# A macaron layer on one core: the planner counts GpSimd's own lengths and turns of two lengths, masks move to VectorE, and the maxima's transposition moves within bare turns

## The chip, the cores and the metric

The kernel runs on one core of a Trainium2 chip, as one launch. The metric is the device time in microseconds. The kernel before took 1269.98 us (median of three runs, 1268.98 to 1270.04). Engines are named as in the profile: PE (matmuls), DVE (VectorE), ACT (ScalarE), POOL (GpSimd) and SP, which here only issues DMAs.

## The reference, cut to what matters

```python
def ffn(x):                       # on 2*1024 tokens of 512
    logits = x @ W_router.T       # 8 experts, best two, weights normalized
    h = einsum('td,erd->ter', x, lora_A)                  # rank 16
    return x @ W_base.T + b_base + einsum('ter,eor,te->to', h, lora_B, w) * 2.0

def bitnet_linear(x, weight, scale):
    s = max(mean(abs(weight), axis=1), 1e-8)
    y = einsum('bsi,oi->bso', x, sign(weight / s[:, None]))
    return nan_to_num(y * (s * scale), nan=0.0, posinf=1e6, neginf=-1e6)

def attn(x):                      # 32 heads, 8 key/value heads, head width 16
    q, k, v = (bitnet_linear(x, ...) for each)
    return bitnet_linear(softmax(q k^T / 4) v, o_weight, o_scale)

x = x + 0.5 * ffn(layernorm(x))
x = x + attn(layernorm(x))
x = x + 0.5 * ffn(layernorm(x))
```

x is 2 x 1024 x 512, all in float32. `nan_to_num` follows each of the four projections. It is computed exactly by `finite`: two clamps, their sum, a mask "y times 0 equals 0" that is false where y is not finite, and a copy of y where the mask is true.

## The kernel before, in words

The tokens of each of the two batches fall into two groups of 512, each four tiles of 128. A group (b, g) goes through a chain of steps: layernorm and transposition (`ln_T`), router and low-rank part, base matmuls (`ffn_tiles`), a second layernorm, the projections (`qkv_part`: i = 0 to 3 are q, 4 is k, 5 is v). q and k go to DRAM as a high and a low part (`qd`, `kd`, stored from L572), v stays in SBUF (`vd`). After attention a group is divided by its sums (`normalize`), projected (`o_proj`) and goes through the second `ffn`. `binarize` makes the weights' signs.

Attention has 32 units: a batch, a block of 512 queries and a key/value head with its four query heads. Each unit takes four **turns**. A turn does, for three successive stages at once, 8 score tiles for the row maxima (m; each a matmul of L776 and a DVE maximum of L784), 8 score tiles for the exponentials (e0 and e1; L811 and L815 on PE, then L818 on ACT) and four pieces of the product with v (A0 to A3; L851). The e tiles of a unit begin five turns after its m tiles. In the first turn after a unit's maxima are complete, `m_place` (the entry S) transposes them on PE (mp, L796), splits them into a high and a low part on DVE (mT, L798 and L799) and sends both over SP into `mq` (L802), which e1 reads (L815) from the next turn on. After the first turn of a unit, `place` loads the next unit's q (k<-qd, L725) and k (k<-kd, L733); that data is used four turns later.

All instructions are put out by one Python program, whose order is the order on every engine. The **planner**, `Flow`, keeps a clock `flow.t` in ticks of 0.115 us. The steps of the groups and the weights are generators, **strands**. A strand yields what it needs next: a kind (P, v, a, g for PE, DVE, ACT, POOL, d for a DMA on SP, r for buffers, u and j for conditions) and the kind of the piece before it. `go` sets its due time `s.at`: the end of the piece before, plus a distance from the table `LATER`, such as gv=30 for DVE after POOL or av=16 for DVE after ACT. `offer(kind)` places the first strand whose piece of that kind is due, in order of rank, unless the engine is still held (`busy`, set ahead by `LASTS` at the ends and by `APART` inside attention; 11 and 10 ticks for POOL).

During attention a turn follows a written order: `LEAD_IN` at first, `FULL` where a PE piece of a strand is due (37 entries, two F entries for such pieces), `BARE` where none is (35 entries and no F). V and W offer DVE, C and D ACT; POOL and SP are offered after every entry, but SP not before S in a turn that has one. Each turn counts `TICK` = 64 ticks. Where something must be done before work goes on, `need` runs `until`: each tick it clears the holds and offers all engines, with no attention work between, till the condition holds. `need` stands before each `place` and asks for the q and k of that unit; for the first unit of batch 1 that is at the end of turn 60. Here this is called the flush. After attention the strands that are left are played out with the table for free engines.

Of the kernel before, what the change touches and what calls it, by code (L numbers as in the profile page):

```python
# [32 lines left out]
def macaron_kernel(ctx: ExitStack, tc: tile.TileContext, x_in, wbT, b_base, wrT, aT, bT,  # L33
# [82 lines left out]
    for t in mqs:  # L116
# [4 lines left out]

    TICK = 64
    LATER = {False: dict(Pv=10, Pa=10, PP=0, vP=36, aP=36, gP=40, va=20, av=16, vg=16, ag=14, gv=30,
                         ga=30, gg=0, vv=0, aa=0, dv=50, dg=50, da=50, dd=0, gd=32, vd=26, ad=26,
                         xd=50, dP=60),
# [1 line left out]
                        gg=0, vv=0, aa=0, dv=26, dg=26, da=26, dd=0, gd=13, vd=8, ad=8, xd=26,  # L129
                        dP=30)}  # L130
    LASTS = dict(P=9, v=6, a=5, g=11, d=5)
    APART = dict(P=0, v=5, a=5, g=10, d=5)

    class Strand:
# [4 lines left out]
    class Flow:  # L139
        def __init__(self):  # L140
            self.t, self.free, self.strands, self.n = 0, True, [], 0
            self.stock = dict(m=3, n=4, t=11, xT=2, xL=2, hT=1, fb=6)
            self.lock = None
            self.busy = dict.fromkeys("Pvagd", 0)

        def spawn(self, gen, rank):
            self.n += 1
# [6 lines left out]
        def go(self, s):  # L154

            if s.kind in LASTS:
                s.last, s.end = s.kind, self.t
            w = next(s.gen, None)
            if w is None:
                s.done = True  # L160
                self.strands.remove(s)
                return
            s.kind, s.arg = w[0], w[1]
            if s.kind in LASTS:
                since = w[2] if len(w) > 2 and w[2] is not None else s.end
                s.banks = w[3] if len(w) > 3 else 0
                s.at = since + LATER[self.free].get(s.arg + s.kind, 0) if s.arg else since
# [30 lines left out]
        def offer(self, kind):  # L198
            if self.t < self.busy[kind]:
                return False  # L200
            self.settle()
            for s in self.strands:
                if s.kind == kind and s.at <= self.t and (
                        kind != "P" or self.lock in (None, s) and s.banks <= self.stock["fb"]):
                    if kind == "P":
                        self.lock = None
                        self.stock["fb"] -= s.banks
                    self.go(s)
                    self.busy[kind] = self.t + (LASTS if self.free else APART)[kind]
                    self.settle()  # L210
                    return True
            return False
# [22 lines left out]
    def finite(y, o, n, fast, back):  # L235


        yield "r", dict(m=1)
        lo = t512(f"lo{n}")
        m = tmp.tile([P, 512], mybir.dt.uint8, tag="mask", name=f"m{n}", bufs=3)  # L240
        lo_, m_ = lo[:, :], m[:, :]
        if len(o.shape) == 3:
            lo_, m_ = (v.rearrange("p (a c) -> p a c", a=o.shape[1]) for v in (lo_, m_))
        src, t = back
        if fast:
            yield "v", src, t
            nc.vector.tensor_scalar(lo_, y, 0.0, -BIG, ALU.min, ALU.max)
            yield "v", "v"
            nc.vector.tensor_scalar(o, y, 0.0, BIG, ALU.max, ALU.min)
            e, eng = ("v", nc.vector) if fast > 1 else ("g", nc.gpsimd)  # L250
            yield e, "v"
            eng.tensor_tensor(o, o, lo_, ALU.add)
            last = e, flow.t
            yield "v", ""
            nc.vector.tensor_scalar(m_, y, 0.0, 0.0, ALU.mult, ALU.is_equal)
        else:
            yield "g", src, t
            nc.gpsimd.tensor_scalar(lo_, y, 0.0, -BIG, ALU.min, ALU.max)  # L258
            yield "g", ""
            nc.gpsimd.tensor_scalar(m_, y, 0.0, 0.0, ALU.mult, ALU.is_equal)  # L260
            yield "g", ""
            nc.gpsimd.tensor_scalar(o, y, 0.0, BIG, ALU.max, ALU.min)
            yield "g", "g"
            nc.gpsimd.tensor_tensor(o, o, lo_, ALU.add)  # L264
            last = "g", flow.t
        flow.give(t=1)
        yield ("v", *last)
        nc.vector.copy_predicated(o, m_, y)  # L268
        flow.give(m=1)
# [9 lines left out]
    def ln_T(xt, n, mv, given, tiles, xs, rank):  # L279


        xT, xL = xs if len(xs) > 1 else (xs[0], None)
        own = slice(tiles[0], tiles[-1] + 1)
        yield "u", lambda: given >= set(tiles)
        yield "v", "v"
        ve = sm.tile([P, TG], F32, tag="ve", name=f"ve{n}{tiles[0]}")
        nc.vector.tensor_scalar(ve[:, own], mv[:, own, 1], EPS, None, ALU.add)
        yield "g", "v"
        rstd = sm.tile([P, TG], F32, tag="rstd", name=f"rstd{n}{tiles[0]}", bufs=4)
        nc.gpsimd.tensor_tensor(rstd[:, own], ve[:, own], mhalf[:, own], ALU.pow)  # L290
        calm = not flow.free
        if calm:
            yield "g", ""
            neg = sm.tile([P, TG], F32, tag="neg", name=f"neg{n}{tiles[0]}", bufs=4)
            nc.gpsimd.tensor_tensor(neg[:, own], mv[:, own, 0], rstd[:, own], ALU.mult)
            yield "g", ""
            nc.gpsimd.tensor_scalar(neg[:, own], neg[:, own], -1.0, None, ALU.mult)
        at = flow.t

        def part(t):  # L300
            yield "r", dict(t=1)
            yield "a" if calm else "v", "g", at
            xn = t512(f"xn{n}_{t}")
            if calm:
                nc.scalar.activation(xn, xt[:, t, :], AF.Identity, bias=neg[:, t:t + 1],
                                     scale=rstd[:, t:t + 1])
            else:
                nc.vector.tensor_scalar(xn, xt[:, t, :], mv[:, t, 0:1], rstd[:, t:t + 1],
                                        ALU.subtract, ALU.mult)
            yield "P", "a" if calm else "v", None, 1  # L310
            pt = bank(f"pt{n}_{t}").rearrange("p (c q) -> p c q", c=KC)
            for c in range(KC):
                nc.tensor.transpose(pt[:, c, :], xn[:, c * P:(c + 1) * P], ident)
            flow.give(t=1)
            yield "a", "P"
            tok = slice(t * P, (t + 1) * P)
            nc.scalar.copy(xT[:, :, tok], pt)
            if xL is not None:
                yield "v", "a"
                nc.vector.tensor_tensor(xL[:, :, tok], pt, xT[:, :, tok].bitcast(F32), ALU.subtract)  # L320
            flow.give(fb=1)

        yield "j", [flow.spawn(part(t), rank) for t in tiles]
# [146 lines left out]
    def binarize(w, n_out, name, sc, rank, at):  # L470
# [18 lines left out]
            nc.vector.reciprocal(rs[:, c * P:(c + 1) * P], s[:, c * P:(c + 1) * P])  # L489
        wr = const.tile([P, KC, n_out], F32R, name=f"sign_{name}")  # L490
        for c in range(KC):
            yield "g", "v" if c == 0 else "g"
            nc.gpsimd.tensor_tensor(w[:, c, :], w[:, c, :], rs[:, 0:n_out], ALU.mult)
            g = flow.t
            if c:
                yield "a", "g", was
                nc.scalar.activation(wr[:, c - 1, :], w[:, c - 1, :], AF.Sign)
            was = g
# [149 lines left out]
    def o_proj(b, g, hs, rank, mv, given, fast=False):  # L648
# [5 lines left out]
        def part(t):  # L654
# [20 lines left out]
                yield "g", "a"  # L675
                nc.gpsimd.tensor_tensor(y, y, osc, ALU.mult)
            r = t512(f"ro{n}_{t}")
            yield from finite(y[:, :], r[:, :], f"o{n}_{t}", fast, ("v" if fast else "g", flow.t))
            yield "v" if fast else "g", "v"
            (nc.vector if fast else nc.gpsimd).tensor_tensor(xt[:, t, :], xt[:, t, :], r, ALU.add)  # L680
            flow.give(t=2)
# [5 lines left out]
        for t in range(TG):  # L687
# [10 lines left out]
    FULL = ("V F W m0(3) e0(4) e0(7) e0(1) m0(7) e1(4) e1(7) e1(1) A0 A1 S C e0(5) e0(3) e1(5) "  # L698
            "e0(2) m0(4) V e1(2) m0(0) e1(3) A2 A3 m0(2) e0(0) C e0(6) m0(5) e1(6) e1(0) m0(6) D "
            "m0(1) F")  # L700
    BARE = ("A0 A1 S e0(1) C m0(7) e1(1) e0(3) e0(4) e0(2) m0(0) e1(3) e1(2) C e1(4) m0(2) m0(5) A2 "
            "A3 m0(3) e0(0) V e0(6) D e1(0) e0(7) e0(5) e1(6) m0(1) e1(7) V e1(5) W m0(6) m0(4)")
    LEAD_IN = ("m0(0) m0(5) m0(2) V m0(7) F C V m0(4) m0(1) V F C m0(6) V F C V m0(3) V S F C V")
    FULL, BARE, LEAD_IN = (
# [50 lines left out]
    def place_v(u):  # L755

        b, _, g = units[u]
        v = p2.tile([P, NT, 32], F32, tag="vaug", name=f"vaug{u}", bufs=3)
        nc.gpsimd.memset(v[:, :, HD:32], 1.0)
        nc.gpsimd.tensor_copy(v[:, :, 0:HD], vd[b][:, :, g * HD:(g + 1) * HD])  # L760
        st[u]["v"] = v
# [99 lines left out]

    def attention(chains, n0):

        start = flow.t
        flow.free, flow.lock = False, None
        flow.busy = dict.fromkeys("Pvagd", flow.t)
        flow.stock["fb"] -= 4
# [14 lines left out]
            raise RuntimeError([(s.rank, s.kind, s.arg) for s in flow.strands])  # L882

        for n in range(n0, TU * len(units) + LEAD + 1):
            begin = flow.t = max(flow.t, start + (n - n0) * TICK)
            m, e, a = todo(n, 0), todo(n, LEAD), todo(n, LEAD + 1)
            live = [c for c in live if not c.done]
            while chains and len(live) < 3 and chains[0][0] <= n:
# [1 line left out]
            if e and e[1] == 0:  # L890
                need(*[(units[e[0]][0], h, KC + 1) for h in range(NG)])
                place_v(e[0])
            order = (LEAD_IN if not e and not a else FULL if flow.wants("P", begin + at_F)
                     else BARE)

            hold = n % TU == 0 and n // TU
            for pos, (kind, p, i) in enumerate(order):
                flow.t = max(flow.t, begin + pos * TICK // len(order))
                if kind == "m":
                    if m:  # L900
                        m_tile(m[0], m[1] * 2 * REP + i)
# [25 lines left out]
            if m and m[0] + 1 < len(units) and (m[1] == 0 or n == n0):  # L927
                b, qb, g = units[m[0] + 1]
                need((b, qb, g // 2), *[(b, h, KC) for h in range(NG)])
                place(m[0] + 1)  # L930
        flow.free = True
        flow.stock["fb"] += 4
        flow.busy = dict.fromkeys("Pvagd", flow.t)

# [51 lines left out]

    def chain_o():
        yield from binarize(wraw["o"], D, "o", osc, 8, usec(36))
        load_x(1, 1)

    def have(*keys):
# [67 lines left out]
```

## Time and profile before

| | |
|---|---|
| median of three runs | 1269.98 us (1268.98 to 1270.04) |
| profiled execution | 1269.39 us, span 1267.6 us |
| mean granted PE clock | 0.923 |
| instructions | 21528 |
| HBM read, written | 51.19 MB, 25.94 MB |
| m, e and av tiles' matmuls (L776, L811, L815, L851) | 367.2, 284.8, 261.4, 284.7 us busy |
| DVE maxima (L784) | 649.7 us, 1024 of 682 ns |
| ACT exponentials (L818) | 543.8 us, 1024 of 604 ns |

A row of the groups gives line, engine, operation, result and source, shapes and count, then busy time, the mean of one in ns, and the idle time just before it with what ended it. A busy PE is modelled and includes its pipelining. In the slices a digit is tenths of a fortieth of the span, 31.7 us. The chain that ended last is followed back from the last instruction to whatever released each step.

### The profile page before, as it was taken

How to read it: one execution, taken by the hardware profiler on the slowest of the kernel's cores; microseconds unless marked ns; L12 is line 12 of the kernel's file. 1: busy time of each engine (PE TensorE's matmuls, PEld its weight loads, DVE VectorE, ACT ScalarE, POOL GpSimd, SP SyncE). 2: the span in 40 equal slices, each digit the busy share in tenths (PEclk: the TensorE clock that was granted, in tenths of full speed). 3: DMA queues.
4: the chain of work that ended last, by engine and by line, in shares of the span. 5: the costliest groups of instructions: out<-in, count | busy, mean ns of one | idle time of the engine just before them, and what ended most of it. 6: DMA issues, size and time to landing. Idle time of an engine off the chain costs nothing.

```text
span 1267.6 us, 21528 instructions
## 1 busy us (share of the span) xinstructions
PE 1085.7 (86%) x8453; PEld 599.8 (47%) x8453; DVE 857.5 (68%) x1644; ACT 666.3 (53%) x1305; POOL 400.2 (32%) x387
## 2 busy tenths in 40 slices
PE   3977368999999999988658898999998799989868
PEld 3535234555454554444434454544455345545434
DVE  6575646787777777776245885787778567785373
ACT  2221135776567566656245575656575466677501
POOL 4232954300110271040785603471110030921201
PEclk8988568999999999999869898999999899999889
DMA  7011113211111122122113122111112211111111
GB/s 251 1 63 46 44 43 115 85 52 48 45 47 47 44 84 68 43 71 84 51 44 107 56 75 81 48 42 59 54 52 69 79 67 52 61 52 45 42 35 41
DMA packets 43089, 79.04 MB, mean 62 GB/s; under 512 B 7259, under 2 KB 10331, under 8 KB 42987
## 3 DMA queue, kind: packets, MB, share of 16 engines
q1 hardware_dynamic: 41578, 74.97, 16.9%
q10 hardware_dynamic: 1152, 2.10, 0.4%
q8 instruction: 67, 1.10, 0.4%
q0 software_dynamic: 256, 0.59, 0.3%
q14 instruction: 36, 0.29, 0.1%
HBM read 51.19 MB, written 25.94 MB: 61 GB/s over the span
## 4 chain that ended last, share of the span: by engine, by line
PE 59%; DMA 12%; DVE 11%; issue 8%; POOL 5%; SPq 2%; ACT 2%; POOLq 0%; DVEq 0%; ACTq 0%
PE av L851 16%; PE m L776 13%; PE e L811 8%; DMA k<-kd 8%; PE e L815 6%; DVE mn L784 4%; PE pbf L438 4%; PE pbs L438 3%; PE po L663 2%; POOL ma L260 1%; PE pq L532 1%; ACT es L818 1%; DMA an<-ad 1%; DMA x<-in_x 1%; SPq L725 1%
## 5 line engine op out<-in xcount | busy, mean ns | idle before, releaser
L784 DVE TENSOR_REDUCE mn<-m 128x1 f32<-128x512 f32 x1024 | 649.7, 682 | 244.5 <-PE e L815 100.8
L818 ACT ACTIVATE es<-e 128x512 f32<-128x512 f32 x1024 | 543.8, 604 | 343.1 <-PE e L815 295.1
L776 PE MATMUL m<-k 64*128 64x512 f32 x1024 | 367.2, 450 | 75.2 <-DMA k<-kd 40.6
L811 PE MATMUL e<-k 64*128 64x512 f32 x1024 | 284.8, 454 | 22.6 <-ACT es L818 20.0
L851 PE MATMUL av<-es,vaug 128*32 128x256 f32 x4096 | 284.7, 397 | 20.2 <-issue 8.0
L776 PEld LDWEIGHTS m<-k 64*128 64x128 f32 x1024 | 173.3, 193 | 219.6 <-DVE mn L784 81.9
L815 PE MATMUL e<-mq,two_r 64*128 64x512 f32 x1024 | 261.4, 407 | 2.5 <-DMA mq<-mT 2.5
L851 PEld LDWEIGHTS av<-es,vaug 128*32 128x32 f32 x4096 | 110.1, 111 | 156.6 <-issue 103.6
L811 PEld LDWEIGHTS e<-k 64*128 64x128 f32 x1024 | 123.7, 191 | 78.8 <-DVE mn L784 30.6
L815 PEld LDWEIGHTS e<-mq,two_r 64*128 64x128 f32 x1024 | 149.6, 193 | 15.8 <-POOL ma L260 2.9
L615 POOL TENSOR_TENSOR an<-an,rb 128x512 f32<-128x512 f32 x15 | 19.6, 1308 | 175.7 <-DMA rb<-rd 140.3
L438 PE MATMUL pbf<-wb,xTf 128*128 128x512 f32 x128 | 65.0, 638 | 0.0
L453 POOL TENSOR_TENSOR x<-x,hbf 128x512 f32<-128x512 f32 x8 | 10.2, 1280 | 164.7 <-ACT hbf L450 164.7
L438 PE MATMUL pbs<-wb,xTs 128*128 128x512 f32 x128 | 61.4, 606 | 0.1
L433 POOL TENSOR_TENSOR x<-x,bh 128x512 f32<-128x512 f32 x32 | 40.9, 1304 | 0.0
L258 POOL TENSOR_SCALAR loa<-y 128x512 f32<-128x512 f32 x17 | 12.9, 762 | 88.3 <-ACT y L537 87.7
L438 PEld LDWEIGHTS pbf<-wb,xTf 128*128 128x128 f32 x128 | 24.3, 202 | 28.7 <-issue 27.5
L565 POOL TENSOR_TENSOR z<-z,y 128x512 fp32r<-128x512 f32 x17 | 21.6, 1274 | 49.8 <-ACT y L562 47.2
L268 DVE COPY_PREDICATED z<-ma,y 128x512 f32<-128x512 uint8 x20 | 19.0, 950 | 25.4 <-POOL z L264 25.2
L438 PEld LDWEIGHTS pbs<-wb,xTs 128*128 128x128 f32 x128 | 22.7, 189 | 27.3 <-issue 26.4
L453 POOL TENSOR_TENSOR x<-x,hbs 128x512 f32<-128x512 f32 x8 | 10.3, 1282 | 79.4 <-ACT hbs L450 79.4
L562 ACT CAST y<-z 128x512 fp32r<-128x512 f32 x20 | 12.5, 623 | 41.6 <-DVE z L268 40.3
(210 smaller groups left out, 1098.7 us busy)
## 6 DMA issues: line engine op xcount, KB each, us to landing
k<-qd SPq DMA_DIRECT2D x128, 128.0 KB
k<-kd SPq DMA_DIRECT2D x31, 512.0 KB
ad<-avs SPq DMA_DIRECT2D x32, 256.0 KB
x<-in_x SPq DMA_DIRECT2D x16, 256.0 KB
qd<-y SPq DMA_DIRECT2D x16, 256.0 KB
qd<-z SPq DMA_DIRECT2D x16, 256.0 KB
an<-ad SPq DMA_DIRECT2D x15, 256.0 KB
rb<-rd SPq DMA_DIRECT2D x15, 256.0 KB
```

The costliest lines, as they stand in the source:

```text
L433: nc.gpsimd.tensor_tensor(xt[:, t, :], xt[:, t, :], bh, ALU.add)
L438: nc.tensor.matmul(pb, xT[:, c, t * P:(t + 1) * P], wb[:, c, :], start=(c == 0), stop=False)
L453: nc.gpsimd.tensor_tensor(xt[:, t, :], xt[:, t, :], hb, ALU.add)
L565: (nc.vector if fast else nc.gpsimd).tensor_tensor(lo, o, y, ALU.subtract)
L615: nc.gpsimd.tensor_tensor(z, z, rb, ALU.mult)
L663: nc.tensor.matmul(po, hs[j][:, c, t * P:(t + 1) * P], wo[:, c, :], start=(c + j == 0), stop=(c + j == KC))
L776: nc.tensor.matmul(s["m", i], s["q"][rows_of(h), h % 2, qt * P:(qt + 1) * P], s["k"][rows_of(h), kh * 512:(kh + 1) * 512], start=True, sto ...
L784: nc.vector.tensor_reduce(s["mn"][:, h, qt, kh:kh + 1], s.pop(("m", i)), AX.X, ALU.max, negate=True)
L811: nc.tensor.matmul(t, s["k"][rows_of(h), kt * P:(kt + 1) * P], s["q"][rows_of(h), h % 2, :], start=True, stop=False)
L815: nc.tensor.matmul(t, two_r[rows_of(h), h % 2, :], s["mq"][rows_of(h), :], start=False, stop=True)
L818: nc.scalar.activation(e, s.pop(("e", i)), AF.Exp, scale=HD ** -0.5)
L851: nc.tensor.matmul(s["av"][32 * h:32 * h + 32, cols], s["v"][:, kt, :], s["es"][kt * REP + h][:, cols], start=(kt + half == 0), stop=(kt + ...
```

## The change

1. The planner counts POOL's queue. `Flow.pool` is the tick at which all that is placed on POOL has ended. Every POOL piece adds its own length, given as a fourth value of its yield (6, 17, 9, 3, 4), else `SUM` = 11. The strand's own end becomes `pool - SUM`, and POOL is offered again only when `pool` is reached. The distances of later pieces (`last`, `at`, `g`) count from there too.
2. In `finite`, where it isn't one of the fast forms, the mask moves from POOL to DVE and stands between the two clamps in the strand's order.
3. A bare turn counts `BRIEF` = 50 ticks; full and leading turns keep 64. Each turn's begin follows from the one before, and not from the number of the turn; after attention the clock is set to the last turn's end.
4. In `BARE`, S moves from the third to the seventeenth entry.
5. `chain_o` yields for a place on SP before it loads the x of group (1, 1).

```diff
-    TICK = 64
+    TICK, BRIEF = 64, 50
...
+    SUM = 11
...
+            self.pool = 0
...
             if s.kind in LASTS:
                 s.last, s.end = s.kind, self.t
+            if s.kind == "g":
+
+                self.pool = max(self.pool, self.t) + (s.banks or SUM)
+                s.end = self.pool - SUM
...
-                    self.busy[kind] = self.t + (LASTS if self.free else APART)[kind]
+                    self.busy[kind] = (self.pool if kind == "g" else
+                                       self.t + (LASTS if self.free else APART)[kind])
...
-            last = e, flow.t
+            last = e, flow.t if e == "v" else flow.pool - SUM
...
-            yield "g", src, t
+            yield "g", src, t, 6
             nc.gpsimd.tensor_scalar(lo_, y, 0.0, -BIG, ALU.min, ALU.max)
-            yield "g", ""
-            nc.gpsimd.tensor_scalar(m_, y, 0.0, 0.0, ALU.mult, ALU.is_equal)
-            yield "g", ""
+            yield "v", src, t
+            nc.vector.tensor_scalar(m_, y, 0.0, 0.0, ALU.mult, ALU.is_equal)
+            yield "g", "", None, 17
             nc.gpsimd.tensor_scalar(o, y, 0.0, BIG, ALU.max, ALU.min)
             yield "g", "g"
             nc.gpsimd.tensor_tensor(o, o, lo_, ALU.add)
-            last = "g", flow.t
+            last = "g", flow.pool - SUM
...
-        yield "g", "v"
+        yield "g", "v", None, 9
         rstd = sm.tile([P, TG], F32, tag="rstd", name=f"rstd{n}{tiles[0]}", bufs=4)
...
-            yield "g", ""
+            yield "g", "", None, 3
             neg = sm.tile([P, TG], F32, tag="neg", name=f"neg{n}{tiles[0]}", bufs=4)
...
-        at = flow.t
+        at = flow.pool - SUM
...
-            yield "g", "v" if c == 0 else "g"
+            yield "g", "v" if c == 0 else "g", None, 11 if n_out > P else 4
             nc.gpsimd.tensor_tensor(w[:, c, :], w[:, c, :], rs[:, 0:n_out], ALU.mult)
-            g = flow.t
+            g = flow.pool - SUM
...
-    BARE = ("A0 A1 S e0(1) C m0(7) e1(1) e0(3) e0(4) e0(2) m0(0) e1(3) e1(2) C e1(4) m0(2) m0(5) A2 "
+    BARE = ("A0 A1 e0(1) C m0(7) e1(1) e0(3) e0(4) e0(2) m0(0) e1(3) e1(2) C e1(4) m0(2) m0(5) S A2 "
             "A3 m0(3) e0(0) V e0(6) D e1(0) e0(7) e0(5) e1(6) m0(1) e1(7) V e1(5) W m0(6) m0(4)")
...
         v = p2.tile([P, NT, 32], F32, tag="vaug", name=f"vaug{u}", bufs=3)
+        flow.pool = max(flow.pool, flow.t) + 5
...
-        start = flow.t
+        begin, span = flow.t, 0
...
-            begin = flow.t = max(flow.t, start + (n - n0) * TICK)
+            begin = flow.t = max(flow.t, begin + span)
...
+            span = BRIEF if order is BARE else TICK
...
-                flow.t = max(flow.t, begin + pos * TICK // len(order))
+                flow.t = max(flow.t, begin + pos * span // len(order))
...
         flow.free = True
+        flow.t = begin + span
...
         yield from binarize(wraw["o"], D, "o", osc, 8, usec(36))
+        yield "d", "x"
         load_x(1, 1)
```

More of the change, by code (lines that the diff above doesn't have):

```diff
@@ L292, in ln_T @@
         if calm:
-            yield "g", ""
+            yield "g", "", None, 3
             neg = sm.tile([P, TG], F32, tag="neg", name=f"neg{n}{tiles[0]}", bufs=4)
             nc.gpsimd.tensor_tensor(neg[:, own], mv[:, own, 0], rstd[:, own], ALU.mult)
-            yield "g", ""
+            yield "g", "", None, 3
             nc.gpsimd.tensor_scalar(neg[:, own], neg[:, own], -1.0, None, ALU.mult)
-        at = flow.t
+        at = flow.pool - SUM
         def part(t):
@@ L677, in part @@
             r = t512(f"ro{n}_{t}")
-            yield from finite(y[:, :], r[:, :], f"o{n}_{t}", fast, ("v" if fast else "g", flow.t))
+            yield from finite(y[:, :], r[:, :], f"o{n}_{t}", fast,
+                              ("v" if fast else "g", flow.t if fast else flow.pool - SUM))
             yield "v" if fast else "g", "v"
```

## The prediction

> **What bounds the kernel now.** I read the page first, then the chain that ended last, then that chain and the POOL queue in the two stretches where the 40 slices dip, and last the rows of the operations that the change moves. The page's busy shares and slices:
>
> ```profile
> PE 1085.7 (86%) x8453; PEld 599.8 (47%) x8453; DVE 857.5 (68%) x1644; ACT 666.3 (53%) x1305; POOL 400.2 (32%) x387
> PE   3977368999999999988658898999998799989868
> DVE  6575646787777777776245885787778567785373
> POOL 4232954300110271040785603471110030921201
> ```
>
> PE is busy 86%, and in long stretches all the time; there a cheaper POOL is worth nothing. PE falls to 3 to 6 tenths in slices 5 and 6 and again around slices 20 and 21, and exactly there POOL reads 9, 5, 8, 5. POOL's 32% over the whole span hides two stretches in which it is the bound. The same by stage (columns: PE, PEld, DVE, ACT, POOL busy, clock, DMA):
>
> ```profile
> 100.00:170.00 70.00, 37.61 (x159) 24.38 (x160) 38.34 (x66) 9.52 (x18) 46.84 (x35) 0.67 0.13 43
> 170.00:546.00 376.00, 359.09 (x3011) 193.20 (x3010) 280.43 (x516) 238.23 (x460) 78.19 (x84) 0.96 0.17 60
> 546.00:660.00 114.00, 79.93 (x610) 46.17 (x604) 58.77 (x99) 53.17 (x100) 62.36 (x50) 0.82 0.19 63
> 660.00:1180.00 520.00, 471.69 (x4091) 257.78 (x4091) 378.93 (x704) 323.00 (x630) 166.56 (x159) 0.96 0.18 63
> ```
>
> PE lacks 32 us in 100 to 170, 34 us in 546 to 660 and 48 us in 660 to 1180. In the second of these the chain that ended last runs through POOL, one `finite` after another (start, length, what):
>
> ```profile
> 615.45 1.95 POOL ma L260
> 617.47 1.93 POOL z L262
> 619.48 1.29 POOL z L264
> 620.85 1.13 POOL loa L258
> 622.04 1.93 POOL ma L260
> ...
> 641.62 1.93 POOL ma L260
> 643.61 1.92 POOL z L262
> 645.62 1.27 POOL z L264
> 646.91 1.77 DVE z L268
> ```
>
> This is the flush: after turn 60 `need` wants k and q of batch 1, and the planner puts all of their remaining pieces ahead of turn 61. DVE's copy and ACT's next work stand in order behind POOL, so PE gets nothing. From 120.06 to 141.58 the chain holds four more masks; the SP queue, which must then send q to DRAM, issues unit 1's k at 146.90 and that lands 20.7 us later. So nine masks lie on the path, 1.4% of the span (17.5 us). The rows that the change moves:
>
> ```profile
> L260 POOL TENSOR_SCALAR ma<-y 128x512 uint8<-128x512 f32 x17 | 32.9, 1935 | 1.0
> L260 POOL TENSOR_SCALAR mo<-yo 128x512 uint8<-128x512 f32 x12 | 23.2, 1934 | 0.6
> L255 DVE TENSOR_SCALAR ma<-y 128x512 uint8<-128x512 f32 x3 | 1.2, 415 | 0.0
> L796 PE MATMUL mp<-ident,mm 128*16 128x128 f32 x32 | 9.5, 297 | 13.9 <-DVE mm L789 13.9
> ```
>
> **The masks.** With the four of `vd`, 33 masks leave POOL: 33 x 1.935 = 63.9 us. They cost DVE 33 x 0.415 = 13.7 us. POOL's part of a `finite` shrinks from 0.61 + 1.93 + 1.92 + 1.27 = 5.73 to 3.80 us. Only masks on the path count: four at the start, five in the flush.
>
> Against the full 1.93 stands a rule of the Trainium skill, SBUF — State Buffer, section "Who interferes with whom": a VectorE tensor_scalar from SBUF to SBUF in its two-port mode and a GpSimd instruction exclude each other, and whichever comes second waits for the whole of the first. The trace has such meetings: the DVE `lo` at 63.31 took 1.43 us while POOL ran w_q, against 0.41 without company, and the copy at 646.91 above 1.77 beside POOL's L565, against a median of 0.74. By the POOL row alone the nine masks give 9 x 1.93 = 17.4 us; by the rule POOL is shut out for each mask, 9 x (1.93 - 0.42) = 13.6 us. I take the rule's: start 4 x 1.51 = **-6.0**, flush 5 x 1.51 = **-7.6**.
>
> Off those two places a mask costs DVE. In full turns DVE has room (14.5 of 20 us busy around 300), and PE, busy for all 20, hides it. In bare turns, 5.6 to 6.0 us long, eight maxima of 0.682 fill 5.46 us, so there a mask is on the path. The planner's list for the kernel before has 90 full and 37 bare of the 127 turns from 6 on. If masks fall evenly, 24 x 37/127 = 7 meet a bare turn, at 0.42 to 1.43 us: 3 to 10 us. **+5**, as not every mask meets POOL at work.
>
> **POOL's own lengths.** Before, a POOL piece holds its engine for 10 or 11 ticks of 0.115 us and is thought done at once; a `finite` is planned at 40 ticks, 4.6 us, and takes 5.73. In the flush the holds are even set to zero, so all five `finite`s are placed before the first k part's last subtraction (L565, at 646.84). After, each further piece of a strand is due only when the counted POOL queue is done, and a `finite` counts 6 + 17 + 11 = 34 ticks, 3.9 us. The first k part then needs 30 + 20 + 14 = 64 ticks to its subtraction, room for two other `finite`s and not four. The flush should hold one `finite` less: **-3.8** (none if the order stays; two, -7.6). At the start the q store on SP is planned at a truer time too, so the k load behind it can go sooner: **-2** (0 to -10: k's own store was issued by 121.9, q1's at 142.9). The smaller lengths (w at 4, pow at 9, vaug at 5) bring earlier offers worth nothing where POOL sat idle.
>
> **Turns of two lengths.** A bare turn counts 50 ticks (5.75 us) instead of 64 (7.36). Measured bare turns without a wait are 5.6 to 6.0, so 50 is right, and strands' due times hold. Before, they were offered too soon, and in-order queues stood: after the flush, the turns 68, 70, 84 and 102 lasted 4.2, 2.8, 3.5 and 2.8 us over their kind, 13.3 in all. Half of it gone is **-6.5** (0 to -13). Before the flush the same gain is worth nothing: a turn reached sooner waits at `need` for the same chain. The price is in the strands: 14 bare turns before `need` hold 14 x 14 = 196 ticks less, 22.5 us. Where the chain's end is set by latency in real time, that is zero, and I take zero; where it isn't, see the rival.
>
> **The transposition.** In bare turns S moves from the third to the seventeenth place of the order, past four maxima tiles, eight halves of score tiles and two places for ACT. Nine S turns are bare. PE stood 13.9 us at L796 for the gather, eight times; with S later it works on: at best -14. What moves with it: mp (0.28), two DVE copies (0.28 each, now behind up to four maxima), two SP issues of 0.6 us and their landing, 1.70 us in the chain. After S 18 of 35 places of a bare turn are left, 3.0 us, and the first e that reads mq comes 2 to 2.5 us into the next turn; the path is 0.3 + 1.0 + 0.6 + 1.2 + 1.7 = 4.8 against about 5.2, so it just fits, with up to 1 us of wait in each (+9). SP holds other DMAs until S, and the next unit's k (21 us to land) goes out behind mq, 2 us later; turns 64, 76 and 108, each four after a bare S turn, already wait 7, 7 and 13 us for such a load (+6). Between -14 and +15: **-3**, since DVE, whose idle is what counts, gets only part of PE's time.
>
> **The x load of (1,1)** becomes an offered piece, four DMAs on SP. The queue stood 0.5 us for them at 198.2; nothing reads them for 80 us: 0. The filling after attention starts at a counted time: 0.
>
> **Sum**, against the profiled execution, 1269.39 us (span 1267.6, 1.8 around it): -6.0 - 7.6 + 5 - 3.8 - 2 - 6.5 - 3 = -23.9, so 1245.5. The median of the runs is 0.6 higher: **1246 us**.
>
> **Rivals.** (a) *Loads swallow it.* Unit 1's k waits for its own 20.7 us, and three turns already wait for k loads; faster bare stretches run into the same loads. For it: L776 waited 40.6 us for k in the page's idle column. Only the flush's 11.4 and half of the start's 6.0 remain, less 5 for DVE: 1270 - 9.4 = 1261.
> (b) *The chain falls behind*; slower. POOL's `o` now waits for the mask's place among the two or three V places of a turn, and due times pass in fewer ticks per turn, so at `need` the chain of batch 1 lacks pieces that used to lie beside attention. They run in the flush with PE idle: 196 ticks, +22.5. After the flush, 22 more bare turns push 308 ticks, about five turns' ten PE pieces (0.95 us each), behind the last turn: +9.5. With -24 that makes +8; if the gains of order (3.8, 2 and 6.5) fail too, +20: 1278 to 1290. It decides once the flush, 155 ticks before, passes about 155 + 24/0.115 = 364 ticks. Against it: latency in real time doesn't grow with a tick count.
> (c) *The lock eats the masks.* Each of 33 waits about 1.4 us on DVE and holds maxima behind it: in seven bare turns 10, in the flush and start nothing gained: 1246 + 5 + 13.6 = 1265. The two meetings speak for it; against it, the median copy of 0.74, though POOL is busy for much of each chain.
>
> **Chances and range.** A run of this kernel tells 0.2%, 2.5 us. The forecast's case (1230 to 1258) 0.48, with a larger gain, if the start's loads and both order gains come whole, 0.08 (1210 to 1230); (a) and (c) together 0.15, a quarter of it within 0.2%; (b) 0.29, nearly all slower. So faster 0.67, same 0.05, slower 0.28. For 8 in 10 I leave 0.06 below 1216 and about 0.1 above 1288; the forecast's own range is 1230 to 1258.
>
> **What the next profile shows.** Right: no L260 row on POOL, a DVE row of 33 at 0.42 to 0.6 us; POOL in the flush two or three us per `finite` shorter; turn 61's gap below 30 us (35 over its kind before); L796's idle below 5. Wrong: a mask row above 1 us; a longer gap at the second batch; more idle at L815 for mq; more leftover pb work after the last av. The forecast fails above all if the flush grows.

## The result: slower, and the profile after

The changed kernel took 1284.77 us (median of four runs, 1284.07 to 1288.96) against 1270.01 beside it: a ratio of 1.0121, 95% interval 1.0096 to 1.0146. The forecast was 1246 us with 0.28 for slower. The profiled execution took 1285.31 us with a span of 1283.5. Its lines are numbered seven to nine higher: maxima L793, mq's matmul L824, the k load L741, `normalize`'s load of the sums rs<-ad L608, their reciprocal L614. Busy time and slices of the page after:

```profile
PE 1095.9 (85%) x8453; PEld 606.0 (47%) x8453; DVE 881.8 (69%) x1677; ACT 667.6 (52%) x1305; POOL 337.6 (26%) x354
PE   3987557899999999978679878999998599998788
DVE  6675676677877777777367866688677478973393
POOL 4233850200002041131564402143020113401321
```

POOL lost 63 us of work and DVE gained 24, but the kernel ends 16 us later. The same by stage, the middle bounds set to the flush of this kernel (columns as before):

```profile
100.00:170.00 70.00, 43.98 (x177) 29.36 (x179) 39.19 (x68) 11.52 (x21) 39.30 (x31) 0.70 0.18 59
170.00:549.00 379.00, 351.06 (x2953) 189.17 (x2954) 283.25 (x523) 233.40 (x451) 60.18 (x75) 0.96 0.16 56
549.00:657.00 108.00, 82.89 (x650) 48.87 (x642) 64.14 (x107) 55.26 (x104) 44.14 (x40) 0.87 0.22 72
657.00:1180.00 523.00, 469.19 (x4028) 252.99 (x4027) 376.82 (x680) 315.89 (x612) 131.53 (x134) 0.95 0.16 58
```

PE lacks 25 us in the stage of the flush (34 before), but 28 instead of 17 in the stage ahead of it and 54 instead of 48 behind. The end of each turn, read from its eighth e matmul with mq in both timelines, gives the ledger (after minus before):

| stretch | us |
|---|---|
| start to the end of turn 5 | +3.0 |
| turns 6 to 60 | +7.6 |
| turn 61, with the flush in front of it | -13.9 (42.4 to 28.5) |
| turns 62 to 129 | +9.7 |
| turns 130 to 132 | +4.8 |
| what is left after the last turn | +4.6 |

The flush did what was forecast. POOL's timeline there (start, length, line, operation, and the idle time before it), first the two ends of the stretch in the kernel before:

```profile
614.77 0.61 POOL L258 TENSOR_SCALAR loa<-y 128x512 f32<-128x512 f32 x1 [6.61 <-ACT y L537]
646.84 1.26 POOL L565 TENSOR_TENSOR z<-z,y 128x512 fp32r<-128x512 f32 x1
```

and then in the changed one:

```profile
626.75 0.61 POOL L265 TENSOR_SCALAR loa<-y 128x512 f32<-128x512 f32 x1 [5.79 <-ACT y L544]
627.45 1.92 POOL L269 TENSOR_SCALAR z<-y 128x512 f32<-128x512 f32 x1
630.34 0.72 POOL L265 TENSOR_SCALAR loa<-yv 128x512 f32<-128x512 f32 x1 [0.98 <-DVE yv L561]
...
635.82 0.94 POOL L265 TENSOR_SCALAR loa<-y 128x512 f32<-128x512 f32 x1
...
642.82 1.73 POOL L572 TENSOR_TENSOR z<-z,y 128x512 fp32r<-128x512 f32 x1
```

From the first k part's lower clamp to its last subtraction 17.8 us pass (33.3 before), and two other `finite`s lie between, where there were four.

The waits show where the time went. Two rows before and the same two in the changed kernel (engine, line, what it waited for: us in total, times, longest):

```profile
PE m L776 <- DMA k<-kd: 40.6, 7, 18.1
DVE rs L607 <- DMA rs<-ad: 3.9, 2, 3.4
```

```profile
PE m L785 <- DMA k<-kd: 56.2, 10, 13.3
DVE rs L614 <- DMA rs<-ad: 28.9, 3, 15.4
```

The second is new in size. DVE's reciprocal of a group's sums stands for its load; DVE takes its instructions in the order of the program, so the maxima behind the reciprocal stand too, and then PE. The longest of these waits lies in turn 107, 22.1 us long. SP's queue there:

```profile
980.60 1.22 SPq L811 DMA_DIRECT2D mq<-mT  x2
981.88 0.61 SPq L608 DMA_DIRECT2D rs<-ad  x1
982.54 0.59 SPq L612 DMA_DIRECT2D an<-ad  x1
983.17 0.57 SPq L608 DMA_DIRECT2D rs<-ad  x1
983.78 0.57 SPq L612 DMA_DIRECT2D an<-ad  x1
984.40 0.57 SPq L608 DMA_DIRECT2D rs<-ad  x1
985.01 0.57 SPq L612 DMA_DIRECT2D an<-ad  x1
985.68 3.65 SPq L733 DMA_DIRECT2D k<-qd  x4
989.37 2.51 SPq L741 DMA_DIRECT2D k<-kd  x1
991.93 5.04 SPq L608 DMA_DIRECT2D rs<-ad  x1
```

and DVE:

```profile
994.93 0.69 DVE L793 TENSOR_REDUCE mn<-m 128x1 f32<-128x512 f32 x1 [2.94 <-PE m L785]
1011.03 0.35 DVE L614 RECIPROCAL rs<-rs 128x32 f32<-128x32 f32 x1 [15.41 <-DMA rs<-ad]
```

and what PE waited for meanwhile, a transposition behind a maximum:

```profile
PE pts L320 <- DVE mn L793: 15.0, 2, 14.7
```

Turn 104 is bare and has S. SP is offered nothing before S; with S late, 28 of the turn's 50 ticks are left (an expectation below says 26), and the planner counts 5 for a DMA, so six DMAs fit before `place` puts out the next unit's q and k. The fourth load of sums goes out right behind the k load, and its reciprocal starts 19.1 us after the issue began; the three ahead took 4.5 to 5 us. The trace's DMA packets show where this load stood: of its 128 packets of 128 bytes, 96 had moved by 998.14 us, and the last 32 moved from 1010.21 to 1010.42, right after the k load's last packet of 4096 bytes had ended at 1010.27. All three waits of DVE above 4 us in this profile, in turns 60, 76 and 107, are for an rs<-ad issued within 3.1 us of a k<-kd.

### The profile page after: what moved, and what is told of

Read it like the earlier page. It is cut to its first block, busy times and chain, and to the rows that moved or that the text cites. A ratio compares the mean times of both kernels' runs of the same rounds, so it can differ in the third digit from the quotient of the medians.

```text
span 1283.5 us, 21548 instructions
## 1 busy us (share of the span) xinstructions
PE 1095.9 (85%) x8453; PEld 606.0 (47%) x8453; DVE 881.8 (69%) x1677; ACT 667.6 (52%) x1305; POOL 337.6 (26%) x354
## 5 line engine op out<-in xcount | busy, mean ns | idle before, releaser
L793 DVE TENSOR_REDUCE mn<-m 128x1 f32<-128x512 f32 x1024 | 650.4, 683 | 229.9 <-PE e L824 108.6
L785 PE MATMUL m<-k 64*128 64x512 f32 x1024 | 370.3, 450 | 78.8 <-DMA k<-kd 56.2
L860 PE MATMUL av<-es,vaug 128*32 128x256 f32 x4096 | 287.8, 400 | 24.7 <-ACT es L827 8.1
L824 PE MATMUL e<-mq,two_r 64*128 64x512 f32 x1024 | 261.4, 405 | 8.1 <-DMA mq<-mT 8.1
L824 PEld LDWEIGHTS e<-mq,two_r 64*128 64x128 f32 x1024 | 148.6, 191 | 20.9 <-issue 8.6
L683 POOL TENSOR_TENSOR yo<-yo,osc 128x512 f32<-128x512 f32 x12 | 15.4, 1283 | 117.4 <-ACT yo L678 89.6
L622 POOL TENSOR_TENSOR an<-an,rb 128x512 f32<-128x512 f32 x15 | 19.1, 1273 | 103.4 <-DMA rb<-rd 103.2
L440 POOL TENSOR_TENSOR x<-x,bh 128x512 f32<-128x512 f32 x32 | 42.4, 1350 | 0.5 <-DVE xns L315 0.4
L572 POOL TENSOR_TENSOR z<-z,y 128x512 fp32r<-128x512 f32 x17 | 22.1, 1302 | 62.0 <-ACT y L569 47.4
L269 POOL TENSOR_SCALAR z<-y 128x512 f32<-128x512 f32 x17 | 34.1, 2006 | 8.3 <-DMA qd<-y 7.1
```

Source lines behind the costliest of these rows:

```text
L440: nc.gpsimd.tensor_tensor(xt[:, t, :], xt[:, t, :], bh, ALU.add)
L572: (nc.vector if fast else nc.gpsimd).tensor_tensor(lo, o, y, ALU.subtract)
L622: nc.gpsimd.tensor_tensor(z, z, rb, ALU.mult)
L785: nc.tensor.matmul(s["m", i], s["q"][rows_of(h), h % 2, qt * P:(qt + 1) * P], s["k"][rows_of(h), kh * 512:(kh + 1) * 512], start=True, sto ...
L793: nc.vector.tensor_reduce(s["mn"][:, h, qt, kh:kh + 1], s.pop(("m", i)), AX.X, ALU.max, negate=True)
L824: nc.tensor.matmul(t, two_r[rows_of(h), h % 2, :], s["mq"][rows_of(h), :], start=False, stop=True)
```

## The experiments

Theory A: the late S, through the hold on SP, pushes loads behind the k load. Theory B: S is worth what was forecast, and the loss lies elsewhere. Theory C: with a short k load the kernels would hardly differ. Rival (b): shorter turns make the chains lag. (The first four expectations call the lag 1, the late loads 2 and the mask's place 3.) All kernels compute the whole reference. Ratios are to the kernel before, timed beside them.

**Each part undone.** u_no_brief: `TICK, BRIEF = 64, 64`. u_s_back: S at its old place. u_masks_back, and the core of u_no_pool, in which the ends count from the clock again:

```diff
-            yield "v", src, t
-            nc.vector.tensor_scalar(m_, y, 0.0, 0.0, ALU.mult, ALU.is_equal)
+            yield "g", "", None, 17
+            nc.gpsimd.tensor_scalar(m_, y, 0.0, 0.0, ALU.mult, ALU.is_equal)
```

```diff
-            if s.kind == "g":
-
-                self.pool = max(self.pool, self.t) + (s.banks or SUM)
-                s.end = self.pool - SUM
...
-                    self.busy[kind] = (self.pool if kind == "g" else
-                                       self.t + (LASTS if self.free else APART)[kind])
+                    self.busy[kind] = self.t + (LASTS if self.free else APART)[kind]
```

> The changed kernel with 64 ticks for every turn, all else as changed. Theory 1 (lag: shorter bare turns give the strands too little planned time, so that work is left for the ends): most of the 15 us come back, 1262 to 1272 us. Theory 2 (loads: the loss lies in PE's waits for k<-kd, 56.2 us after against 40.6 before, because S and the DMAs that it holds back on SP go out later in bare turns): 1279 to 1287. Theory 3 (the mask's place: each finite now waits for a place of DVE among the turn's few, and the chains end later): 1280 to 1288.

> The changed kernel with S at its old third place in bare turns. The plan is otherwise the same, turn for turn. Theory 2 (loads go out late because of S): 1268 to 1276 us, and PE's waits for k<-kd back to some 42 us. Theories 1 and 3: 1282 to 1290, since S does only what the forecast gave it, -3 us.

> The changed kernel with the masks of the slow finite back on GpSimd, counted there at 17 ticks. Theories 1 and 2: the flush loses the gain of the masks again, 1290 to 1300 us. Theory 3 (the mask's place makes the chains late): flush +8 to +14, but the later chains end sooner, -10 to -15; 1276 to 1286.

> The changed kernel without the counted POOL queue: holds of 10 or 11 ticks and a strand's end at its placing, as before; masks on VectorE, two turn lengths and the late S stay. All three theories: the flush keeps the shorter finites but loses the order's gain of 3.8 us, and the first stretch its 2: 1286 to 1293 us. Were the counting itself the cost (later due times for every strand): 1270 to 1280.

| undone in the changed kernel | us | ratio, 95% |
|---|---|---|
| nothing | 1284.77 | 1.0121 (1.0096 to 1.0146) |
| two turn lengths | 1264.95 | 0.9937 (0.9912 to 0.9962) |
| late S | 1262.51 | 0.9929 (0.9906 to 0.9953) |
| masks on VectorE | 1282.30 | 1.0082 (1.0059 to 1.0106) |
| counted POOL queue | 1286.07 | 1.0098 (1.0061 to 1.0134) |

Taking away either the late S or the short turns makes the rest faster than before. DVE's waits for rs<-ad go with either: 28.9 us fall to 2.5 with one turn length and to 4.7 with the old S, but stay at 27.5 and 33.0 with the masks back or the count gone. For S the plan has the same full and bare turns, so the 22 us belong to its place alone. The waits with the old S, and the SP queue at the same turn 104:

```profile
PE m L785 <- DMA k<-kd: 57.1, 8, 13.4
DVE rs L614 <- DMA rs<-ad: 4.7, 1, 4.7
```

```profile
967.62 0.57 SPq L608 DMA_DIRECT2D rs<-ad  x1
968.23 0.57 SPq L612 DMA_DIRECT2D an<-ad  x1
968.90 4.14 SPq L733 DMA_DIRECT2D k<-qd  x4
973.09 2.55 SPq L741 DMA_DIRECT2D k<-kd  x1
```

The fourth rs<-ad is ahead of k and its reciprocal runs at 977.42, 9.8 us after the issue. The part of the expectation that k waits would fall to 42 us failed: they stay at 57. So the late S didn't cost by a late k load. The masks hardly matter in the sum, and theory 3's range was met: back on POOL they make turn 61 15.2 us longer (28.5 to 43.7) and the start and turns 6 to 60 together 11.2 us shorter. Nor does the count: without it turn 61 is 11.6 us longer and turns 6 to 60 are 8.9 us shorter.

**Each part alone** in the kernel before; the edits are those of the diff.

> The kernel before with nothing but S moved to the seventeenth place of bare turns; the plan is that of before, turn for turn. Theory A (the hold: SP is offered nothing before S, so in a bare turn with a late S the loads of normalize, rs<-ad above all, go out behind the next unit's k loads, and DVE's reciprocal then stands for them with all maxima behind it; 28.9 us of such waits in the changed kernel, 4.7 with S back): two of the nine bare turns with S, 56 and 104, lie where a group is divided, so PE gains up to 10 us at the transposition and loses 10 to 20 there: 1268 to 1282 us, and DVE's wait for rs<-ad goes above 10 us. Theory B (the forecast: S is worth -3 by itself, and its cost in the changed kernel is an accident of that kernel's order): 1262 to 1270, rs waits below 6.

> The kernel before with nothing but the masks of the slow finite moved to VectorE, in the old planner. By the forecast's terms -6.0 - 7.6 + 5: 1261 us. If the mask's place among DVE's few places makes the chains late (the second ffn of group (1,0) is then left almost whole for the end): 1270 to 1280.

> The kernel before with nothing but the counted POOL queue, masks still on GpSimd at 17 ticks. By the forecast's terms (order in the flush -3.8, first stretch -2): 1264 us. If true lengths stretch the flush in the plan (288 ticks in place of 155 here) and in time: 1278 to 1295.

> The kernel before with nothing but 50 ticks for bare turns. By the forecast's term: -6.5, 1263 us. By rival (b) (the chains lag, the flush takes 238 ticks in place of 155, more is left for the end): 1278 to 1290.

| alone | us | ratio, 95% |
|---|---|---|
| late S | 1273.31 | 1.0022 (1.0008 to 1.0036) |
| masks on VectorE | 1265.34 | 0.9969 (0.9951 to 0.9987) |
| counted POOL queue | 1273.51 | 1.0025 (1.0010 to 1.0040) |
| two turn lengths | 1291.91 | 1.0168 (1.0140 to 1.0195) |

The late S alone costs 0.2%. PE's idle at the transposition goes from 13.9 us to almost none,

```profile
PE mp L796 <- DVE mn L784: 0.2, 1, 0.2
```

rs waits stay at 4.1, and k waits rise from 40.6 to 51.0. So theory A's number failed here: with 64 ticks, 35 are left after a late S, and the loads got out. The place of S and the length of the turn work together. The masks gain about half of what was forecast; turn 61 falls by 10.8 us (42.4 to 31.6). The count alone takes 7.2 us off turn 61, though the plan's flush grows to 288 ticks, but puts 7.4 us on turns 6 to 60 and 7.1 on turns 62 to 129; neither expectation was met, and why those turns grow is not shown. The short turns alone are rival (b): the flush in the plan takes 238 ticks for 155, turn 61 lasts 56.9 us, and rs waits are 16.0 us.

**The hold, and the load itself.** after_hold:

```diff
-                if not hold:
+                if not hold or order is BARE:
                     flow.offer("d")
```

In the chain of before the k load, 512 KB, takes 20.7 us, and a 256 KB store takes 4.61:

```profile
80.52 4.61 DMA qd<-z
146.90 20.70 DMA k<-kd
```

The Trainium skill, DMA: Bandwidth & Descriptors, section "Rules for kernel authors", says that a leading broadcast of c copies confines a DMA to at most c of the 16 engines; the load's source is `[2, 64, s]` with a broadcast 2. The trace agrees: while only k's packets move, two are under way at nearly any time. That is a share of 0.13 of the 16 DMA engines, the last number but one of this row of the kernel before:

```profile
158.00:167.00 9.00, 0.00 (x0) 0.00 (x0) 0.00 (x0) 0.00 (x0) 8.84 (x8) 0.50 0.13 52
```

So, in after_ksplit, before_ksplit and sback_ksplit (the changed kernel, the one before, and the changed one with S at its old place):

```diff
-        nc.sync.dma_start(st[u]["k"].bitcast(F32)[:, s0:s1],
-                          kd[b][g * 64:(g + 1) * 64, s0:s1].unsqueeze(0).to_broadcast(
-                              [2, 64, s1 - s0]))
+        for h in range(2):
+            nc.sync.dma_start(st[u]["k"].bitcast(F32)[64 * h:64 * h + 64, s0:s1],
+                              kd[b][g * 64:(g + 1) * 64, s0:s1])
```

> The changed kernel with one condition altered: in bare turns DMAs are offered before S too. Order on all engines but SP stays. Theory A (the hold: with the late S only 26 ticks are left for DMAs before the next unit's loads, so an rs<-ad goes out right behind k<-kd and lands 19 to 20 us later): the waits of DVE for rs<-ad fall from 28.9 us to below 8, turn 107 loses its 22 us, 1262 to 1274 us. Theory B (the loss with the late S lies at mq and k, which stay late): 1279 to 1288.

> The changed kernel with the k load as two DMAs of 64 rows each in place of one whose leading dimension is a copy of two; the plan is the same, turn for turn. Theory C (all that differs between these kernels after the start is how much work stands behind a k load of 20 us; made short, it takes the cost of the late S and of the order away): PE's waits for k<-kd fall from 56 us to below 10, rs waits from 29 to below 6, 1205 to 1230 us. If the load isn't limited by its shape, the k load stays at some 20 us: 1283 to 1288.

> The kernel before with the k load as two DMAs of 64 rows. Theory C: k waits from 41 to below 8 us, 1225 to 1240; the changed kernel with the same load is then the faster of the two, by the shorter flush (14 us) less what its chains leave for the end (5 us): by 5 to 20 us. If the changed order is worse by itself (lag, work left for the end): the changed one stays slower, by 5 to 15.

> The changed kernel with S at its old place and the k load as two DMAs of 64 rows. Theory C: with short k loads the place of S is worth little, within 5 us of the changed kernel with the same load, the late S the better by what PE waits at the transposition (some 15 us of idle, part of it on DVE's path). If S hurts by something else than DMAs behind k: 15 to 25 us faster than with the late S.

| kernel | us | ratio, 95% |
|---|---|---|
| after_hold | 1267.35 | 0.9978 (0.9963 to 0.9993) |
| after_ksplit | 1204.03 | 0.9473 (0.9424 to 0.9522) |
| before_ksplit | 1208.27 | 0.9516 (0.9478 to 0.9553) |
| sback_ksplit | 1192.20 | 0.9390 (0.9347 to 0.9433) |

Releasing the hold, with S still late, gives 17 of the 22 us back, and rs waits fall:

```profile
DVE rs L614 <- DMA rs<-ad: 4.7, 1, 4.7
```

Theory A holds in the changed kernel; where the other 5 us lie is not shown. The same k load of unit 1 with two DMAs in before_ksplit, from its chain, and the DMA share while most of it moves:

```profile
145.24 13.10 DMA k<-kd
149.00:151.00 2.00, 0.00 (x0) 0.00 (x0) 2.00 (x4) 0.00 (x0) 1.92 (x3) 0.50 0.88 226
```

Like the 20.70 us of before, this begins with the issue on SP behind four q loads; the other half of k is issued 2.4 us later. The packets tell the two parts of each time. Before, q's packets (2048 bytes) move until 157.26 us and k's 128 from 156.97 to 167.20: half of the 20.7 us is the q loads in front, two packets at a time as well. With two DMAs 112 of k's 128 packets move from 148.42 to 151.27, at a DMA share of 0.88 or 14 engines, beside q's; the last 16 move from 156.66 to 158.41, as q's end at 157.12. So the halves do use more engines, and what is left of the 13.1 us is the q loads. (The packets are listed without their engine; this is read from their sizes, counts and times.) PE's waits for k fall from 56.2 to 16.5 us in the changed kernel and from 40.6 to 17.9 in the one before; both times are below the expected ranges, though the waits are above the 10 and 8 us expected. With the same short load the two differ by 4 us, in favour of the changed one; by their intervals that isn't clear. That is less than the 5 to 20 expected. Against theory C, the late S still costs 12 us with a short load. Waits of after_ksplit:

```profile
PE m L785 <- DMA k<-kd: 16.5, 4, 8.9
DVE rs L614 <- DMA rs<-ad: 11.2, 2, 8.9
```

Its longest rs wait is again in turn 107, behind k, now 10.8 us from issue to reciprocal.

**What was open.** nb_ksplit is u_no_brief, o_brief_ksplit is the short turns alone, each with the short k load. hold_ksplit is after_hold with it. hold_kqsplit adds the same for q:

```diff
-                nc.sync.dma_start(q.bitcast(F32)[64 * h:64 * h + 64, t, :],
-                                  qd[b][row:row + 32, qb * 512:(qb + 1) * 512].unsqueeze(0)
-                                  .to_broadcast([2, 32, 512]))
+                for c in range(2):
+                    nc.sync.dma_start(q.bitcast(F32)[64 * h + 32 * c:64 * h + 32 * c + 32, t, :],
+                                      qd[b][row:row + 32, qb * 512:(qb + 1) * 512])
```

> The changed kernel with DMAs offered before S in bare turns and the short k load. If the hold is all that the late S costs: 1186 to 1196 us, level with or ahead of the old S with the same load (1192), rs waits below 3 us. If S itself costs: 1200 to 1206.

> The changed kernel with 64 ticks for every turn and the short k load; S is late, the hold as it was. With long loads 64 ticks took 20 us off. If the shorter turns cost only by the DMAs that they push behind a k load: what is left is the rs wait of 9 us, 1192 to 1201 us against 1204. If the chains' lag costs by itself: 1180 to 1190.

> The kernel before with 50 ticks for bare turns and the short k load, against 1208 us for 64 ticks with the same load. If only loads made the 22 us: 1205 to 1212. If the lag makes most of it (the flush is 14.5 us longer and 5 us more are left for the end in the profile with long loads): 1224 to 1232.

> As hold_ksplit, with the q load, whose leading dimension is a copy of two as well, in two DMAs of 32 rows each. If what PE still waits for at k (16.5 us after the short k load) is the queue of q loads in front: another 5 to 15 us off, 1175 to 1190, with k waits below 8 us. If SP's time to send eight DMAs is the limit: 1188 to 1200.

| kernel | us | ratio, 95% |
|---|---|---|
| hold_ksplit | 1191.43 | 0.9370 (0.9349 to 0.9391) |
| nb_ksplit | 1199.03 | 0.9423 (0.9405 to 0.9441) |
| o_brief_ksplit | 1222.37 | 0.9617 (0.9590 to 0.9643) |
| hold_kqsplit | 1174.95 | 0.9234 (0.9212 to 0.9256) |

hold_ksplit is level with the old S, with no rs wait at all: with short loads the hold was all that the late S cost. The short turns, in the sum and with short loads, cost 5 us (1204.03 against 1199.03, not clear by their intervals), where they cost 20 with long loads; so most of the 20 came by the long loads. Alone they still cost 14 us over before_ksplit, the size of their longer flush (56.9 us for turn 61 in the profiles with long and with short loads). Beside the counted queue and the masks turn 61 lasts 27 to 29 us with either length. In hold_kqsplit k no longer stands behind q for long: of a k load issued from 544.3 us on, all 128 packets move from 545.59 to 548.28. hold_kqsplit beats the kernel before by 7.7% and the changed one by 8.5%. Its page, and then its row of waits for k; one for rs<-ad is no longer there:

```profile
PE 1067.8 (91%) x8453; PEld 592.0 (50%) x8453; DVE 879.9 (75%) x1677; ACT 666.3 (57%) x1305; POOL 338.8 (29%) x354
PE   3989669999999999999799999999999999997778
```

```profile
PE m L785 <- DMA k<-kd: 8.9, 1, 8.9
```

## Why the prediction was wrong, step by step

**The transposition** is the step that failed. Its terms were PE's idle at L796 (-14), mq's path (+9) and a later k load (+6). It said that SP holds other DMAs until S and then followed only the unit's own k behind mq. What was held was the normalize loads, which it put at nothing: 17.4 us by after_hold, as they then stand behind a k load of 20 us. The trace before had the parts: DVE waited 3.4 us for rs<-ad in turn 56, and rs loads issued 7 to 11 us after a k load came to their reciprocal 12 to 20 us later (one 39). Of the terms that were named, o_s alone gives: PE's idle at the transposition -13.7, the wait for mq unchanged (2.5 us before, 2.4 after, where +9 was allowed), the waits for k +10.4 for +6. Their sum, -3.4, is about the forecast's -3, yet o_s is 0.2% slower; what took the gain back there is not shown.

**Turns of two lengths**, -6.5: wrong sign, alone and in the sum, where it is the other half of the same failure. The step priced strands that are offered too soon, and left out that DMAs are counted in the same ticks: 50 instead of 64 takes two or three DMA places out of a turn, and leaves six after a late S where there were seven. Rival (b) was right about the short turns alone: with 238 ticks the flush lost 14.5 us. Its threshold of 364 ticks was no measure: the sum was slower at 185 ticks, with a shorter turn 61, and the count alone had 288 with a shorter turn 61 too.

**The masks and POOL's lengths in the flush**, -7.6 and -3.8: -13.9 measured for turn 61, with two `finite`s between, as the ticks had said, where the sum counted one less. The masks' and the reciprocals' rows on DVE:

```profile
L267 DVE TENSOR_SCALAR ma<-y 128x512 uint8<-128x512 f32 x17 | 9.3, 546 | 1.1 <-ACT y L544 1.1
L267 DVE TENSOR_SCALAR mo<-yo 128x512 uint8<-128x512 f32 x12 | 8.5, 705 | 15.3 <-POOL yo L683 15.3
L614 DVE RECIPROCAL rs<-rs 128x32 f32<-128x32 f32 x15 | 5.0, 340 | 28.9 <-DMA rs<-ad 28.9
```

Means of 0.55 and 0.71 us instead of 0.415: VectorE waits, by a few tenths on average (single masks took up to 1.52), so rival (c)'s 1.4 us for each was far off. The price taken from the port rule was too high for POOL: its upper clamp of the q and k parts went from 1.93 to 2.01, so POOL lost 0.08 and not 0.42 a mask. (Of the two meetings that the forecast cited, the copy at 646.91 was a copy under a mask, not the operation that the rule names.) The second row shows a cost that was left out: one wait of 15.3 us, in turn 130, in which DVE stood for POOL's yo product, because the mask sits in DVE's queue.

**The start**, -6.0 and -2: +3.0. POOL did get through its fourth `finite` 8 us sooner (at 138.2 instead of 146.2 us), but SP's queue now had two pairs of q stores, issued from 132.79 to 143.32, where there had been one. The second half of unit 0's k went out between them at 137.79 instead of 127.11, and unit 1's k at 148.44 instead of 146.90. The place on the path was read right; that a new order may spend the gain was given no price.

**What is left for the end** was put into rival (b) alone. After_hold has the short flush and few waits for rs<-ad, and is still only level with the kernel before (profiled 1270.2 us): +2.9 at the start, +5.2 in turns 6 to 60, -14.8 in turn 61, -2.1 to 129, and +9.7 for turns 130 to 132 and the rest. By the planner's list, before leaves the last base matmuls of group (1, 0), after nearly its whole second `ffn`. It takes the masks and the short turns together: each of the eight kernels that have both shows the 15.3 us wait of DVE in its profile and loses 8 to 11 us after turn 129; in u_no_brief, nb_ksplit, u_masks_back and o_masks, each without one of the two, there is no such wait, and 2.4 to 3.9 us are lost. How much of the loss is that wait is not shown. The place on SP for the x load of (1, 1) was not tried alone.

**Rival (a)**, loads that swallow the gain, named the right resource, but put the kernel only 15 us above the forecast, where 39 were measured: it foresaw the waits for k and not what stands behind k in the queue.

## What to carry to other kernels

A DMA that is moved or held also moves against every other DMA of its queue: list what was issued in the held stretch, and what big transfer it now stands behind. A wait for a small load holds up all that stands behind it on the same engine, so look at small loads whose consumers sit among the main loop's instructions. And look at a transfer's rate before tuning around it: 512 KB in 20.7 us, against 256 KB in 4.6, pointed to a load on two engines, and splitting it was worth 5% by itself, four times all that the change moved.

## What the runs showed of the hardware

In the changed kernel a 16 KB load issued within about 3 us of the 512 KB k load came to its reciprocal 19 to 20 us later, others after as little as 4.5; of the one before turn 107 a quarter of the packets moved only when k's were done. The load whose leading dimension is a broadcast of two had two packets under way at a time and took 20.7 us as one DMA, half of it behind q loads of the same kind; as two DMAs without the broadcast it took 13.1 us, and 112 of its 128 packets moved within 2.9. With k and q loads split as well (after_hold to hold_kqsplit), PE's waits for k went from 56.3 us to 8.9, and the whole kernel's mean granted PE clock from 0.932 to 0.968.
